# Layer 0 self attention: key norms and choice rounds in three pieces, two padding rows, rotation ahead of the output's norm, the next stage's second norm tile by tile

## The chip, the core and the metric

The kernel runs on one core of a Trainium2 chip. TensorE (PE) does the matrix products, with weight loads shown apart as PEld; VectorE (DVE), ScalarE (ACT) and GpSimd (POOL) do the rest; transfers are issued by SyncE (SP). The metric is the time of one execution in microseconds (us), as the median of several. A difference of about 0.3% is what a measurement of this kernel can tell from none.

## The reference, cut to what matters

A two-layer perceiver on `x` (64 batches of 32 rows of 256: 2048 rows) with a context of 64 x 257 rows of 64. Each layer is cross attention, self attention and a feed-forward part; each reads a layer norm of `x` and adds its result to `x`. The change lies in layer 0's self attention and in what is prepared there for later parts.

```python
xn = _layernorm(x, g_norm)          # of a layer-normed x: two norms in a row
q = xn @ Wq ; k, v = split(xn @ Wkv)        # 16 heads of 128, one k and one v
q = l2norm(q * 16) * 4 ; k = l2norm(k) * 4
attn = softmax(q @ k.T) ; out = (attn @ v) @ Wout
x = x + _layernorm(out, g_out)
# layer 0's feed-forward: the 4 likeliest of 16 blocks per row
prob = softmax(xf @ Wr.T + br) ; _, idx = top_k(prob, 4)
h = gelu(xf @ W1.T) * mask(idx) ; y = h @ W2.T
# layer 1's cross attention rotates the context
kv_rope = kv_c * cos + rotate_half(kv_c) * sin
```

## The kernel before, in words

All 2048 rows lie in SBUF as 16 tiles `xs[0]` to `xs[15]` of 128 rows (four batches each); four tiles make a group g = 0 to 3. Stages follow each other: A (layer 0 cross attention), B (layer 0 self attention, lines 845 to 1127), C (feed-forward), then layer 1. All that changes is in stage B, except that `pad` was allocated once for the whole kernel.

**Stage B is a loop over slots t = 0 to 16** (line 1077 on). In it the instructions of PE, DVE, ACT and POOL stand in the order in which the code writes them (`manual_schedule`), and each engine works its own list strictly in that order. The order of the transfers on SP's queue is chosen by the framework's own planner, not by the program text. Slot t does, for its tile:

- `similar(t)`: PE makes the scores `Sb` (L908) and, from the squares `q2b`, the query norms `ssb` (L916); ACT takes the root into `rqb` (L925).
- `gather(t-1)`: PE multiplies the last tile's weights with v into `avb` (L955); DVE and ACT copy two quarters each into `oTb` (L960, L962).
- `scale(t)`: DVE takes the reciprocal `rqb` (L930), then multiplies the scores into `pTb` (L932); `power(t)`: exponential on ACT (L936).
- `square(t+1)`: POOL squares queries of the next tile into `q2b` (L896, four instructions), as soon as ACT has copied them to `qTb` (L885).
- `project(t-1)`: PE, 32 passes into `yb` (L968); `norm_stats(t-1)`: DVE's statistics of `yb` (`lnb_bo`, L174), ACT's root (L980).
- `share(t)`: PE makes the denominators `denb` (L942), DVE their reciprocal `rdb` (L944) and the product `pTb` (L945), which the next slot's `avb` needs.
- `norm_out(t-1)`: DVE's reciprocal (L986) and `ynb` (L992); POOL multiplies by the gain (L993) and adds to `x` (L994).
- `rotate(t)`: nine POOL instructions (L822 to L839) rotate one sixteenth of the context for layer 1; SP stores the results (`ctd` L832, `nad` L840). `fetch(t+1)`: SP loads the next sixteenth (L804 to L812) into tiles with one buffer.
- `write_pad(t)`: DVE fills a row of padding (`pad`, L137 and L138) and SP stores it eight times to `srt` (L140, 1040 KB), for the experts of layer 1.

Four query products `qb` (L877, 8 passes each) per slot, ten ahead of use, fill PE at places 0 to 3. Further work is pinned by hand with `at(slot, place, fn)`: place 5 stands between `power` and `project`, place 3 behind `share`, place 4 behind `fetch`. Pinned there: `keys_norm(g)` (slots 3 and 6, place 5: the two norms in a row of four tiles, for the keys and queries of groups 2 and 3); the choice of blocks: `choose_norm`, `choose_turn`, `choose_blocks`, the four rounds `choose_best` (L679 to L692: largest, equal, first of the equal, strike out) and `choose_store` (PE transposes, L699; DVE copies, L701; SP stores `maskd`, L702); stage C's first hidden group (`hp`, `hc`, L716 to L724, slots 13 to 15) and output (`yc`, L731, L738, slots 15 and 16); and the norm of tiles 4 to 7 for stage C's second group, `ln_group(1, "c")` at slot 15 place 4, turned by `tp_c` (L244) at slot 16.

Helpers: `stats` (L174, L175: two DVE instructions), `ln_out` on ACT (L196), `rstd_of` (L156 to L168: by DVE, an ACT root and a DVE reciprocal, or on POOL by a power of -0.5, L159 and L160).

Of the kernel before, what the change touches and what calls it, by code (L numbers as in the profile page):

```python
# [7 lines left out]
F32 = mybir.dt.float32  # L8
AF = mybir.ActivationFunctionType
ALU = mybir.AluOpType  # L10
# [3 lines left out]
P = 128  # L14
B, S, D = 64, 32, 256
NT = B * S // P
NG = NT // 4
# [8 lines left out]
DP = D + 4  # L26
FE = 1024
EPS = 1e-5
# [19 lines left out]
def perceiver_kernel(ctx: ExitStack, tc: tile.TileContext, a: dict, out: bass.AP):  # L48
    nc = tc.nc


    const = ctx.enter_context(tc.tile_pool(name="const", bufs=1))
# [24 lines left out]
    xs = [x[:, :D] for x in xf]  # L77
# [51 lines left out]
    caus = cst[:, C_CAUS : C_CAUS + S]  # L129
    desc = cst[:, C_DESC : C_DESC + 16]  # L130

    pad = const.tile([P, DP], F32, name="pad")

    def write_pad(n_):


        nc.vector.memset(pad, 0.0)  # L137
        nc.vector.memset(pad[:, D : D + 1], 2.0 * B * S)  # L138
        r0 = n_ * NE * P
        nc.sync.dma_start(  # L140
            srt[r0 : r0 + NE * P].rearrange("(j p) c -> p j c", p=P), bc(pad, 1, NE)
        )
# [4 lines left out]
    mhalf = const.tile([P, 4], F32, name="mhalf")  # L147
# [22 lines left out]
    def stats(mv_slot, src, name, sign=None):  # L170
        st = sm(f"lnb_{name}", [P, 6])
        if sign is not None:
            nc.vector.tensor_copy(st[:, 0:1], sign)
        nc.vector.bn_stats(st, src)  # L174
        nc.vector.bn_aggr(mv_slot, st)  # L175
# [16 lines left out]
    def ln_out(x_, rs, sh, i, name, act=False):  # L192

        y = xnp.tile([P, D], F32, tag="xn", name=f"xn_{name}_{i}")
        if act:
            nc.scalar.activation(  # L196
                y, x_, AF.Identity, scale=rs[:, i : i + 1], bias=sh[:, i : i + 1]
            )
        else:
            nc.vector.scalar_tensor_tensor(  # L200
                y,
                x_,
                rs[:, i : i + 1],
                sh[:, i : i + 1].to_broadcast([P, D]),
                ALU.mult,
                ALU.add,
            )
        return y

    def ln_group(g, name, twice=False, act=False, power=False, sign=None):  # L210

        mv = sm(f"lnm_{name}{g}", [P, 4, 2])
        for i in range(4):
            stats(mv[:, i, :], xs[4 * g + i], f"{name}{g}_{i}", sign)
        rs, sh = ln_scale(mv, f"{name}{g}", twice, power)
        return [ln_out(xs[4 * g + i], rs, sh, i, f"{name}{g}", act) for i in range(4)]
# [132 lines left out]
    def keys_norm(g):  # L349
        latT[g] = ln_group(g, "b", twice=True, act=True, power=g == 0)  # L350
# [324 lines left out]
    def choose_best(g, work, rounds):  # L675

        lg, mx, mask = choice[g]
        for r in rounds:
            nc.vector.tensor_reduce(mx, lg, AX.X, ALU.max)  # L679
            eq = work.tile([P, 4, 16], F32, tag="eq", name=f"eqc{g}_{r}", bufs=1)  # L680
            nc.vector.tensor_tensor(eq, lg, bc(mx, 2, 16), ALU.is_equal)
            nc.vector.tensor_tensor(eq, eq, bc(desc, 1, 4), ALU.mult)
            m2 = sm(f"m2c_{g}_{r}", [P, 4])
            nc.vector.tensor_reduce(m2, eq, AX.X, ALU.max)
            one = mask
            if r:
                one = work.tile([P, 4, 16], F32, tag="one", name=f"onec{g}_{r}", bufs=1)
            nc.vector.tensor_tensor(one, eq, bc(m2, 2, 16), ALU.is_equal)
            if r < 3:
                nc.vector.scalar_tensor_tensor(lg, one, -2.0, lg, ALU.mult, ALU.add)  # L690
            if r:
                nc.vector.tensor_add(mask, mask, one)  # L692

    def choose_store(g, ps, work):

        mask = choice.pop(g)[2]
        mT_ps = ps.tile([16, 512], F32, tag="mm", name=f"mTp{g}")
        for i in range(4):
            nc.tensor.transpose(mT_ps[:, i * P : (i + 1) * P], mask[:, i, :], ident)  # L699
        mT = const.tile([16, 512], F32, tag="mT", name=f"mTc{g}", bufs=1)  # L700
        nc.vector.tensor_copy(mT, mT_ps)  # L701
        nc.sync.dma_start(maskd[g], mT)  # L702
# [23 lines left out]
    def output(g, hs, i, ps, tag, between=lambda f: None):  # L726
        y_ps = ps.tile([P, D], F32, tag=tag, name=f"yc{g}_{i}")
        for f in range(8):
            if f % 4 == 0:
                between(f // 4)  # L730
            nc.tensor.matmul(  # L731
                y_ps,
                hs[f][:, i * P : (i + 1) * P],
                c_2[:, f, :],
                start=(f == 0),
                stop=(f == 7),
            )
        nc.vector.tensor_add(xs[4 * g + i], xs[4 * g + i], y_ps)  # L738
# [106 lines left out]
    with tc.tile_pool(name="wB", bufs=2) as work, tc.tile_pool(  # L845
# [137 lines left out]
        def norm_out(t):  # L983
            y_ps, mv, sd = outs.pop(t)
            rs = sm(f"lnr_bo{t}", [P, 1])
            nc.vector.reciprocal(rs, sd)  # L986

            last = t == NT - 1
            yn = (xnp if last else work).tile(
                [P, D], F32, tag="xn" if last else "yn", name=f"ynb{t}"  # L990
            )
            nc.vector.tensor_scalar(yn, y_ps, mv[:, 0, 0:1], rs, ALU.subtract, ALU.mult)  # L992
            nc.gpsimd.tensor_tensor(yn, yn, vec[:, V_GOUT : V_GOUT + D], ALU.mult)  # L993
            nc.gpsimd.tensor_tensor(xs[t], xs[t], yn, ALU.add)  # L994
# [18 lines left out]

        steps = {}

        def at(slot, place, fn):
            steps.setdefault((slot, place), []).append(fn)

        for g in range(1, NG):
            at(4 * g - 4, 2, lambda g=g: keys_turn(g, ps2))
            slot, place_ = (0, 5) if g == 1 else (4 * g - 3, 1)
            at(slot, place_, lambda g=g: keys_of(g, ps2, 0))
            at(4 * g - 3, 3, lambda g=g: keys_of(g, ps2, 1))
            at(4 * g - 2, 2, lambda g=g: turn_keys(g, ps2))
            if g > 1:
                at((3, 6)[g - 2], 5, lambda g=g: keys_norm(g))
        for g in range(NG - 1):
            at(4 * g + 5, 5, lambda g=g: choose_norm(g))  # L1030
            at(4 * g + 6, 1, lambda g=g: choose_turn(g, ps2, work))
            at(4 * g + 7, 5, lambda g=g: choose_blocks(g, ps2, work))
            if g < NG - 2:
                at(4 * g + 7, 5, lambda g=g: choose_best(g, work, (0, 1)))
            at(4 * g + 8, 5, lambda g=g: choose_best(g, work, (2, 3)))
            if g < NG - 2:
                at(4 * g + 9, 2, lambda g=g: choose_store(g, ps2, work))
        ff, late = {}, []

        def ff_late():  # L1040
# [11 lines left out]

        def ff_output(i):
            output(0, [ff["h"][:, f, :] for f in range(8)], i, ps2, "mm")

        def spread(g):
            mb = []
# [13 lines left out]
        for i, (slot, place) in enumerate(((15, 3), (15, 3), (16, 0), (16, 1))):  # L1071
            at(slot, place, lambda i=i: ff_output(i))
        at(15, 3, lambda: choose_best(NG - 2, work, (0, 1)))
        at(15, 4, lambda: ff.update(xn1=ln_group(1, "c", act=True)))
        at(16, 2, lambda: ff.update(xT1=transposed(ff["xn1"], ps2, 1, "c")))

        for t in range(NT + 1):


            parts = [AHEAD + 4 * t + z for z in range(4)]  # L1080

            def place(z):
                if z < 4:
                    query_part(parts[z])
                for step in steps.get((t, z), ()):
                    step()

            if t < NT:
                similar(t)
            place(0)  # L1090
            if t > 0:
                gather(t - 1)
            if t < NT:
                scale(t)
            place(1)
            square(t + 1)
            ff_late()
            place(2)
            if t < NT:
                power(t)  # L1100
            ff_late()
            place(5)
            if t > 0:
                project(t - 1)
                norm_stats(t - 1)
            if t < NT:
                share(t)
            place(3)
            ff_late()
            if t > 0:  # L1110
                norm_out(t - 1)
            if t < NT:
                rotate(t, work)
            if t + 1 < NT:
                fetch(t + 1, work)
            place(4)
            if t == 2:
                numbers = all_numbers(counted)
                tri, one, token, base = (numbers[z] for z in ("tri", "one", "token", "base"))
                ntile, n128e, n128h = (numbers[z] for z in ("ntile", "n128e", "n128h"))  # L1120
            if t > 2:
                for t_ in {3: (0, 1), NT: (NT - 2, NT - 1)}.get(t, (t - 2,)):
                    nc.gpsimd.tensor_copy(xf[t_][:, D : D + 1], token[:, t_ : t_ + 1])
            write_pad(t)
            if t in (2, 4):
                load_c(t // 4)
        xT_c1 = ff["xT1"]
# [1420 lines left out]
```

## Time and profile before

| | |
|---|---|
| median of 3 runs | 1155.41 us (1152.88 to 1157.0) |
| profiled execution | 1160.48 us, its span 1158.6 us |
| busy share of the span | PE 96%, DVE 66%, ACT 50%, POOL 39% |
| stage B, slots 0 to 16 | 148 to 490 us of the span |
| PE busy in 148 to 490 us | 330.58 of 342 us |

Slot t is counted here from its reciprocal `rqb` on DVE. These start at 148.0, 165.5, 185.3, 206.4, 224.7, 244.4, 266.0, 285.9, 307.6, 327.4, 349.5, 369.3, 390.4, 410.1, 430.0 and 449.7 us (slots 0 to 15); slot 16 has none and is counted from 470. In an instruction line the first number is the start in us, the second the duration; `[x <-E tile L]` says that the engine had been idle for x us and what ended that. In a line of stretches each engine has its busy time and, in brackets, the instructions in it; then come the granted clock of TensorE, the share of DMA time and GB/s.

### The profile page before, as it was taken

What the parts mean: (1) busy time and instruction counts of PE and PEld (TensorE: products, weight loads), DVE (VectorE), ACT (ScalarE), POOL (GpSimd) and SP (SyncE); (2) the same over time, 40 slices, a digit from 0 to 9 for tenths busy, and PEclk for the clock granted to TensorE, in tenths of its full rate; (3) what the DMA queues carried; (4) which work ended last, traced back from release to release, by engine and by line L of the source; (5) the groups of instructions that cost most, each with busy time, mean ns of one, the idle gap of its engine ahead of it and who ended that gap; (6) DMA issues with size and microseconds to landing.
All of it is one profiled execution on the core that took longest, in us unless ns stands there. A gap on an engine that the chain in (4) does not pass through costs nothing. (4 is left out here: it accounts for less than half of the span.)

```text
span 1158.6 us, 26394 instructions
## 1 busy us (share of the span) xinstructions
PE 1106.6 (96%) x10026; PEld 790.2 (68%) x10026; DVE 769.7 (66%) x1812; ACT 575.4 (50%) x1442; POOL 457.0 (39%) x766
## 2 busy tenths in 40 slices
PE   9999999899999999999998999999999989889997
PEld 5667766677767657667676777777777657555653
DVE  5786246868987987765215787777878565765532
ACT  2346363545355365231227777777777456542221
POOL 1444255777768787410001121121222356732111
PEclk9999999999999999999999999999999998989999
DMA  5131132546346446492213121223230044212413
GB/s 133 57 95 40 33 88 85 171 123 168 97 129 206 116 116 191 144 278 69 74 39 66 29 56 29 74 56 83 56 83 19 4 133 126 86 35 74 153 38 118
DMA packets 98990, 109.05 MB, mean 94 GB/s; under 512 B 37240, under 2 KB 73465, under 8 KB 98642
## 3 DMA queue, kind: packets, MB, share of 16 engines
q1 hardware_dynamic: 97138, 103.05, 31.5%
q0 software_dynamic: 1728, 4.33, 1.1%
q8 instruction: 80, 1.31, 0.5%
q14 instruction: 44, 0.36, 0.1%
HBM read 76.36 MB, written 31.41 MB: 93 GB/s over the span
## 5 line engine op out<-in xcount | busy, mean ns | idle before, releaser
L1469 ACT ACTIVATE pp<-Sd,nm 128x256 f32<-128x256 f32 x256 | 119.9, 482 | 40.4 <-POOL nm L1466 40.4
L877 PE MATMUL qb<-xT_b,b_q 128*128 128x256 f32 x512 | 122.2, 386 | 0.8 <-ACT qTb L885 0.8
L877 PEld LDWEIGHTS qb<-xT_b,b_q 128*128 128x128 f32 x512 | 94.9, 191 | 40.1 <-issue 19.3
L1465 DVE TENSOR_REDUCE nm<-Sd 128x2 f32<-128x512 f32 x128 | 79.5, 684 | 54.1 <-PE Sd L1452 54.1
L968 PE MATMUL yb<-b_o,oTb 128*128 128x256 f32 x512 | 114.9, 383 | 0.5 <-DVE oTb L960 0.5
L1466 POOL TENSOR_SCALAR nm<-nm 128x2 f32<-128x2 f32 x128 | 27.0, 211 | 221.6 <-DVE nm L1465 221.3
L968 PEld LDWEIGHTS yb<-b_o,oTb 128*128 128x128 f32 x512 | 97.2, 192 | 14.7 <-issue 1.6
L1487 DVE TENSOR_TENSOR pp<-pp,rd 128x512 f32<-128x512 f32 x128 | 89.6, 700 | 4.4
L1497 PE MATMUL pt<-cst,pp 128*128 128x128 f32 x512 | 68.3, 275 | 6.2 <-DVE pp L1487 5.2
L1503 ACT COPY pTd<-pt 128x512 f32<-128x512 f32 x128 | 68.8, 591 | 10.4 <-PE pt L1497 4.8
L896 POOL TENSOR_TENSOR q2b<-qTb 128x512 f32<-128x512 f32 x64 | 64.7, 1041 | 13.9 <-ACT qTb L885 13.9
L1497 PEld LDWEIGHTS pt<-cst,pp 128*128 128x128 f32 x512 | 59.4, 141 | 15.7 <-ACT ld L1477 5.0
L885 ACT COPY qTb<-qb 128x512 f32<-128x512 f32 x64 | 37.3, 584 | 63.9 <-PE qb L877 61.1
L930 DVE RECIPROCAL rqb<-rqb 128x512 f32<-128x512 f32 x16 | 53.5, 3344 | 17.1 <-ACT rqb L925 17.1
L1245 PE MATMUL qd<-xT_d,d_m 128*128 128x256 f32 x256 | 63.8, 393 | 0.7 <-DVE rd L1486 0.3
L1544 PE MATMUL yd<-d_n,co 128*128 128x256 f32 x256 | 63.2, 391 | 0.0
L1478 POOL TENSOR_TENSOR sd<-sd,ld 128x2 f32<-128x2 f32 x128 | 27.4, 214 | 86.0 <-ACT ld L1477 86.0
L1452 PE MATMUL Sd<-ct,qTd 64*128 64x256 f32 x480 | 60.0, 388 | 0.0
L731 PE MATMUL yc<-c,hc 128*128 128x256 f32 x256 | 58.5, 382 | 0.0
L1518 PE MATMUL od<-pTd,na 128*64 128x256 f32 x480 | 58.4, 385 | 0.0
L1544 PEld LDWEIGHTS yd<-d_n,co 128*128 128x128 f32 x256 | 46.2, 189 | 16.7 <-DVE nm L1465 7.7
L944 DVE RECIPROCAL rdb<-denb 128x512 f32<-128x512 f32 x16 | 53.7, 3354 | 5.8 <-PE denb L942 5.6
(429 smaller groups left out, 2416.8 us busy)
## 6 DMA issues: line engine op xcount, KB each, us to landing
srt<-pad SPq DMA_DIRECT2D x17, 1040.0 KB
mb<-maskd SPq DMA_DIRECT2D x64, 128.0 KB
ct<-ctd SPq DMA_DIRECT2D x30, 257.0 KB
rct<-in_ctxT_dram SPq DMA_DIRECT2D x32, 128.5 KB
rrt<-in_ctxT_dram SPq DMA_DIRECT2D x64, 64.2 KB
ctd<-rct SPq DMA_DIRECT2D x32, 128.5 KB
nad<-rna SPq DMA_DIRECT2D x16, 256.0 KB
fg<-in_f_wg_dram SPq DMA_DIRECT2D x16, 256.0 KB
```

What stands on the lines that cost most here:

```text
L731: nc.tensor.matmul(y_ps, hs[f][:, i * P : (i + 1) * P], c_2[:, f, :], start=(f == 0), stop=(f == 7),)
L877: nc.tensor.matmul(q_ps[:, hh, :], b_q[:, k, h * P : (h + 1) * P], xT[:, k, c0 : c0 + 256], start=(k == 0), stop=(k == KC - 1),)
L896: nc.gpsimd.tensor_tensor(q2[:, 4 * h4 : 4 * h4 + 4, :], q, q, ALU.mult)
L968: nc.tensor.matmul(y_ps, oT[:, h, :], b_o[:, h, :], start=(h == 0), stop=(h == NH - 1))
L1245: nc.tensor.matmul(q_ps[:, r, :], m[:, k, pr * P : (pr + 1) * P], xT[:, k, c0 : c0 + 256], start=(k == 0), stop=(k == KC - 1),)
L1452: nc.tensor.matmul(logits[b][hh][:, u, :], qT[hs, b % 8, 4 * u : 4 * u + 4, :], ct[hs, b % 4, :KEYS], start=True, stop=True,)
L1465: nc.vector.tensor_reduce(nm, s_ps[hh], AX.X, ALU.max, negate=True)
L1469: nc.scalar.activation(pb[:, u, hh, :], s_ps[hh][:, u, :], AF.Exp, bias=nm[:, u : u + 1], accum_out=sd[:, u : u + 1],)
L1487: nc.vector.tensor_tensor(pp, pp, bc(rd, 2, KEYS), ALU.mult)
L1497: nc.tensor.transpose(pts[c][:, hh * 256 + u * P : hh * 256 + u * P + P], probs[b][:, u, hh, c * P : (c + 1) * P], ident,)
L1503: nc.scalar.copy(pT[:, c, :], pt)
L1544: nc.tensor.matmul(y_ps, co[:, pr, :], n[:, pr, :], start=(pr == pr0), stop=(pr == pr0 + n_pr - 1),)
```

## The change: what it does

Six edits, all in stage B:

1. `keys_norm(g)` for g = 2 and 3 becomes `keys_norm_step(g, z)`, one step per slot at place 5: slots 1, 2, 3 for g = 2 and 4, 5, 6 for g = 3. Both roots are taken on POOL (power of -0.5) and no longer on ACT. The last step holds the four `ln_out` on ACT, in the slot where they stood.
2. The four choice rounds of groups 0 and 1 stood two and two in slots 4g+7 and 4g+8; they stand now one, two, one in slots 4g+7, 4g+8, 4g+9. `choose_store` goes from slot 4g+9 to 4g+10, place 2. Group 2 keeps its rounds.
3. `pad` is no longer one row that lives through the kernel, but two rows in turn from stage B's pool.
4. `norm_out(t-1)` stands behind `rotate(t)` and `fetch(t+1)` instead of ahead of them.
5. `ln_group(1, "c")` at slot 15 is taken apart: the statistics of tiles 4 to 7 at place 4 of slots 11 to 14, scale and shift on POOL in slot 14, the four `ln_out` on ACT at slot 15, place 4.
6. The small tiles that must live through several slots come from stage B's pool.

```diff
-    pad = const.tile([P, DP], F32, name="pad")
-    def write_pad(n_):
+    def write_pad(n_, pool):
+        pad = pool.tile([P, DP], F32, tag="pad", name=f"pad{n_}")
         nc.vector.memset(pad, 0.0)
...
+        def keys_norm_step(g, z):
+            if z == 0:
+                mv = work.tile([P, 4, 2], F32, name=f"kbm_{g}", bufs=1)
+                for i in range(4):
+                    stats(mv[:, i, :], xs[4 * g + i], f"b{g}_{i}")
+                r1 = work.tile([P, 4], F32, name=f"kbr_{g}", bufs=1)
+                nc.gpsimd.tensor_scalar(r1, mv[:, :, 1], EPS, None, ALU.add)
+                nc.gpsimd.tensor_tensor(r1, r1, mhalf[:, 0:4], ALU.pow)
+                begun[g] = mv, r1
+            elif z == 1:
+                mv, r1 = begun[g]
+                r2 = work.tile([P, 4], F32, name=f"kbq_{g}", bufs=1)
+                nc.vector.tensor_tensor(r2, mv[:, :, 1], r1, ALU.mult)
+                nc.vector.tensor_tensor(r2, r2, r1, ALU.mult)
+                nc.gpsimd.tensor_scalar(r2, r2, EPS, None, ALU.add)
+                nc.gpsimd.tensor_tensor(r2, r2, mhalf[:, 0:4], ALU.pow)
+                begun[g] = mv, r1, r2
+            else:
+                mv, r1, r2 = begun.pop(g)
+                nc.vector.tensor_tensor(r2, r2, r1, ALU.mult)
+                nc.vector.scalar_tensor_tensor(r1, mv[:, :, 0], -1.0, r2, ALU.mult, ALU.mult)
+                latT[g] = [ln_out(xs[4 * g + i], r2, r1, i, f"b{g}", True) for i in range(4)]
...
-                at((3, 6)[g - 2], 5, lambda g=g: keys_norm(g))
+                for z in range(3):
+                    at((1, 4)[g - 2] + z, 5, lambda g=g, z=z: keys_norm_step(g, z))
...
-            if g < NG - 2:
-                at(4 * g + 7, 5, lambda g=g: choose_best(g, work, (0, 1)))
-            at(4 * g + 8, 5, lambda g=g: choose_best(g, work, (2, 3)))
-            if g < NG - 2:
-                at(4 * g + 9, 2, lambda g=g: choose_store(g, ps2, work))
+            if g == NG - 2:
+                at(4 * g + 8, 5, lambda g=g: choose_best(g, work, (2, 3)))
+                continue
+            for z, rounds in enumerate(((0,), (1, 2), (3,))):
+                at(4 * g + 7 + z, 5, lambda g=g, rounds=rounds: choose_best(g, work, rounds))
+            at(4 * g + 10, 2, lambda g=g: choose_store(g, ps2, work))
...
+        def second_stats(i):
+            if i == 0:
+                for z, shape in (("1m", [P, 4, 2]), ("1r", [P, 4]), ("1h", [P, 4])):
+                    ff[z] = work.tile(shape, F32, name=f"c{z}", bufs=1)
+            stats(ff["1m"][:, i, :], xs[4 + i], f"c1_{i}")
+            if i == 3:
+                rs, sh = ff["1r"], ff["1h"]
+                nc.gpsimd.tensor_scalar(rs, ff["1m"][:, :, 1], EPS, None, ALU.add)
+                nc.gpsimd.tensor_tensor(rs, rs, mhalf[:, 0:4], ALU.pow)
+                nc.gpsimd.tensor_tensor(sh, rs, ff["1m"][:, :, 0], ALU.mult)
+                nc.gpsimd.tensor_scalar(sh, sh, -1.0, None, ALU.mult)
+
+        def second_out():
+            return [ln_out(xs[4 + i], ff["1r"], ff["1h"], i, "c1", True) for i in range(4)]
...
-        at(15, 4, lambda: ff.update(xn1=ln_group(1, "c", act=True)))
+        for i in range(4):
+            at(11 + i, 4, lambda i=i: second_stats(i))
+        at(15, 4, lambda: ff.update(xn1=second_out()))
...
             place(3)
             ff_late()
-            if t > 0:
-                norm_out(t - 1)
             if t < NT:
                 rotate(t, work)
             if t + 1 < NT:
                 fetch(t + 1, work)
+            if t > 0:
+                norm_out(t - 1)
             place(4)
...
-            write_pad(t)
+            write_pad(t, work)
```

## The prediction on record

> **What bounds the kernel now.** The page's busy shares come first: PE 96% of the span, DVE 66%. So the question is where PE stands still. Stage B cut into its slots (start and end, length, then PE, PEld, DVE, ACT, POOL) shows it:
>
> ```profile
> 206.40:224.70 18.30, 15.89 (x80) 11.25 (x81) 17.02 (x31) 8.78 (x16) 11.57 (x13) 1.00 0.60 177
> ...
> 285.90:307.60 21.70, 20.02 (x109) 15.03 (x108) 20.09 (x33) 7.55 (x12) 14.34 (x16) 1.00 0.36 99
> 307.60:327.40 19.80, 19.11 (x99) 13.65 (x98) 18.96 (x27) 8.68 (x13) 15.63 (x18) 1.00 0.45 128
> 327.40:349.50 22.10, 22.10 (x112) 16.32 (x111) 17.09 (x32) 13.19 (x29) 16.89 (x18) 1.00 0.40 114
> ...
> 369.30:390.40 21.10, 19.84 (x108) 14.88 (x107) 19.73 (x33) 7.54 (x12) 14.10 (x16) 1.00 0.54 159
> 390.40:410.10 19.70, 19.36 (x100) 13.87 (x99) 18.86 (x28) 8.50 (x13) 15.53 (x17) 1.00 0.45 127
> 410.10:430.00 19.90, 18.64 (x86) 10.66 (x84) 16.67 (x29) 14.90 (x21) 17.43 (x18) 1.00 0.46 123
> ...
> 470.00:490.00 20.00, 18.67 (x78) 13.27 (x76) 16.62 (x50) 5.38 (x11) 11.57 (x13) 0.91 0.39 123
> ```
>
> These are slots 3, 7, 8, 9, 11, 12, 13, 16. Length minus PE is PE's gap: 2.4 us in slot 3, 1.7 in 7, 1.3 in 11, none in 9. All of stage B holds 342.0 - 330.6 = 11.4 us of gaps, so filling them can win no more. In slots 3, 7, 8, 11 and 12 DVE idles only 0.8 to 1.6 us: it sets the pace there, or nearly. The list of PE's waits in stage B (total, times, longest) names the instruction:
>
> ```profile
> PE avb L955 <- DVE pTb L945: 5.1, 3, 2.2
> PE ssb L916 <- POOL q2b L896: 1.5, 3, 0.8
> PE tp_c L244 <- DVE x L738: 1.0, 1, 1.0
> ```
>
> The three waits of `avb` are in slots 3, 7 and 11: place 5 (`keys_norm(2)`, 210.4 to 217.4; the choice with two rounds in 7 and 11) makes `pTb` late. The same `keys_norm` in slot 6 ends no wait of PE. What a round costs is seen in the timeline of slot 8 (start, duration):
>
> ```profile
> 315.65 1.05 DVE L681 TENSOR_TENSOR eqc<-lgc,mxc 128x64 f32<-128x64 f32 x1
> 316.69 1.26 POOL L839 TENSOR_TENSOR rna<-rna,rlb 128x512 f32<-128x512 f32 x1
> 316.73 1.30 DVE L682 TENSOR_TENSOR eqc<-eqc,cst 128x64 f32<-128x64 f32 x1
> 318.07 0.22 DVE L684 TENSOR_REDUCE m2c<-eqc 128x4 f32<-128x64 f32 x1
> ```
>
> The same L682 takes 0.22 us elsewhere; here it ends as POOL's instruction ends. A DVE instruction with two inputs seems to wait for the POOL instruction under way; the reduction, with one, does not. Slot 8's two rounds hold 9 such instructions, with durations 0.80, 0.65, 0.40, 1.31, 0.21, 1.05, 1.30, 0.84 and 0.96: mean w = 0.84.
>
> **The parts, step by step.** Times are of the profiled execution, 1160.48 us (span 1158.6 and 1.9 around it); that is 5.1 above the median 1155.41, and I carry the difference over to the median.
>
> *Key norms.* Slot 3 loses its seven microseconds at place 5 and keeps two small instructions (0.2 to 1.3 each). `yb` is done at 213.8, `denb` at 214.6; then `rdb` (3.35) and `pTb` (0.69) end by 218.8, before PE arrives at 220.15. The wait goes: **-2.2**. The statistics (four times 0.4 + 0.18 = 2.3) land in slots 1 and 4; in slot 1 DVE idles 5.3 before `lnb_bo`, which hides them, and slot 4 has 8.7 idle in all. Slot 2 idles 5.1; slot 5 gets only two multiplications under a PE that is busy throughout (21.60 of 21.60). Without such cover the 2.3 would be lost twice. POOL adds four times 0.23 + 1.04 (rows L159, L160): in slots 1, 2, 4, 5 `rotate`, `norm_out` and the next `square` queue behind it. POOL idles 89.3 in stage B before `ynb`, so this is covered.
>
> *Choice rounds.* Slot 7 drops a round of 2.8 (297.40 to 300.18): `lnb_bo` moves up to the end of `yb`, and the wait of 1.7 goes; in slot 11 likewise 1.3: **-3.0**. Slots 8 and 12 get rounds 1 and 2 in place of 2 and 3: one striking-out (L690) more, so 10 instructions of w and four reductions of 0.25. From one `avb` to the next `pTb`, DVE's chain in slot 8 was 324.96 - 305.06 = 19.90, 8.49 of it rounds; it becomes 11.41 + 1.0 + 10w = 20.8, against 19.99 from `avb` to `avb`: +0.8. Slot 12 likewise: 407.62 - 388.07 = 19.55, less 8.32, plus 1.0 + 10w: 20.6 against 19.63, +1.0. Slot 13 gets round 3 (4w + 0.5) and slot 12's late statistics (0.6), and loses the copy L701 (0.67): 425.31 - 407.70 = 17.61 becomes 21.4 against 19.91, +1.5. `choose_store` takes PE's 0.6 from a slot that DVE now paces to slot 14, which PE paces: +0.6. Slots 9 and 10, with PE busy 22.10 of 22.10 and 19.56 of 19.80, hide theirs; slot 9's DVE has 5.0 idle for 3.9. Together 24w - 16.25: **+3.9**.
>
> *Rotation ahead of the output's norm.* POOL no longer holds the rotation (10.4 us) until `ynb`, 89.3 us of idling over 16 slots. The squares come next after `norm_out`, ten microseconds earlier, and the waits of `ssb` go: 0.2 in slot 4; the 0.5 and 0.8 in slots 8 and 13 buy nothing where DVE paces. **-0.2**. POOL needs 1.5 + 4.1 + 10.4 = 16.0 of about 20 us per slot. The transfers of `fetch` follow the rotation on SP: 7 us of issue, of which the first rotation needs 3. They start about four microseconds before the next `ynb`, and 5.6 of norm and squares stand ahead of their use: covered. If not, squares have another 8 us before `ssb`.
>
> *Second norm by tiles, end of the stage.* Slot 15 ends with 4.1 us of statistics, ACT's root and shift on DVE (471.08 to 475.17); the `oTb` copies and `x` wait behind them:
>
> ```profile
> 475.21 2.08 ACT L196 ACTIVATE xn_c<-x,lnh_c,lnr_c 128x256 f32<-128x256 f32 x4 [0.93 <-DVE lnh_c L189]
> 476.05 0.62 PE L244 MATMUL tp_c<-cst,xn_c 128*128 128x128 f32 x2 [1.00 <-DVE x L738]
> 478.40 3.77 PE L968 MATMUL yb<-b_o,oTb 128*128 128x256 f32 x11
> ```
>
> With the `xn_c` of ACT made earlier, PE goes from its last `yc` (475.05) through eight transposes (1.1) into `yb` at 476.2: 2.2 less, of which I count 1.6 until the buffers are passed on. And the clock: the next stretch is
>
> ```profile
> 478.00:482.00 4.00, 4.00 (x14) 3.34 (x13) 3.86 (x7) 1.23 (x3) 3.77 (x5) 0.64 0.80 237
> ```
>
> Granted 0.64, just after 1.3 us of gaps in 474 to 478: 4.0 x 0.36 = 1.4 us lost. I count it as filled with the gap: **-3.0** in all. Bounds: -1.6 if the clock falls anyway; -3.6 at best. The four `stats` in slots 11 to 14 (0.6 each) follow `pad`, where DVE waits for `avb` (1.8 idle before `oTb` in slot 14, 1.4 in slot 10); slot 12's is counted above. POOL's two new products lie between 0.2 (L159) and 1.04 (L160), off the path.
>
> The Trainium skill (TensorE: Matmul & The Clock Gate, Part 1) lets the clock fall only after a whole idle window of about 3.4 us; this trace has it fall after 1.3 us of gaps. By that rule the fall has nothing to do with the gap, and the sum would be 1.4 us poorer.
>
> *Two padding rows.* Nothing in stage B waits for the one row's store, so: 0. From above: the last store is issued at 490.13, behind 2 MB of `d_q`. If a tile of stage C lay on the row it would wait for 3 MB at 320 GB/s (490 to 495), some 10 us. By the order of first use, 80 KB of each partition in stage B's pools stand ahead of the row, and stage C's tiles come to 58 KB.
>
> **Sum.** -2.2 - 3.0 + 3.9 - 0.2 - 3.0 = -4.5: the profiled execution 1156.0, the median 1150.9.
>
> **Rivals.**
> A, forecast: 1150.9, own range 1146.3 (w = 0.22, the shortest row, by the same formulas with PE as floor: -9.1) to 1151.9 (0.3% below).
> B, the gaps move: w near 0.95 (losses 6.5) gives -1.9; or new gaps in slots 8, 12 and 13 draw the clock down twice (1.4 each), -1.7. For it: DVE is busy 18.9 of 19.8 in these slots. 1153.5, at most 1158.
> C, slower: the later rounds lie wholly under the rotation, which now begins after the squares. With w = 1.31 (longest row) losses are 24 x 1.31 - 16.25 = 15.2, net +6.8: 1162.2. It decides from w = 1.03 on, and passes 0.3% at 1.17. Against it: slot 8 was already under rotation and squares.
> D, a tile of stage C waits for the padding: -4.5 + 10 = +5.5, 1160.9.
>
> The Trainium skill (SBUF — State Buffer, Who interferes with whom) has the later of two such instructions blocked for the whole of the other. Where each moved instruction meets a fresh POOL instruction this speaks for C.
>
> **Numbers.** A 0.60, B 0.21, C 0.13, D 0.06. Differences over 0.3% are what a measurement of this kernel can tell from none: faster 0.60 (A), same 0.21 (B), slower 0.19 (C, D). The range goes from A's best, 1146.3, to B's end, 1158; C and D stay outside.
>
> **What would show it.** Right: no `avb` wait in slots 3, 7, 11; new ones of about 1 us in slots 8, 12, 13; `ssb` without waits; `ynb` on POOL hardly waited for; clock 1.0 and no `tp_c` wait at the end of the stage. Wrong: mean w over 1.03, a fetch that POOL waits for, a gap of PE at the start of stage C.

## The result, and the profile after

The changed kernel takes 1165.42 us (median of 4 runs, 1164.89 to 1166.73) against 1155.29 us (median of 4, 1152.88 to 1157.0) before: ratio 1.0079, 95% interval [1.0053, 1.0105]. It is **slower by 0.8%**, where 0.4% faster was forecast, and 7 us above the upper end of the range. Its profiled execution took 1165.57 us (span 1163.8). That is only 5.1 above the profiled execution of before, which was 5.2 above its own median; so the comparison is made place by place. The changed kernel has one line less ahead of stage B: L716 of before is L715 here.

TensorE's waits of the changed kernel from 130 to 520 us (total, times, longest):

```profile
PE hp L715 <- ACT hc L722: 6.8, 2, 6.5
PE avb L954 <- DVE pTb L944: 6.5, 3, 3.9
PE yb L967 <- DVE oTb L959: 1.5, 1, 1.5
PE kvp L363 <- ACT qTb L884: 1.1, 1, 1.1
```

The waits of `ssb` and `tp_c` of before are gone, as forecast. But one wait of 6.5 us is new, at `hp`, and the longest at `avb` is now 3.9 where it was 2.2.

The stretches of slots 3, 7, 8, 9, 12, 13, 14 of the changed kernel, counted from `rqb` as before (length, then PE, PEld, DVE, ACT, POOL, granted clock):

```profile
206.96:222.99 16.03, 15.80 (x80) 11.23 (x81) 11.24 (x16) 7.67 (x13) 13.05 (x16) 1.00 0.73 223
283.79:303.56 19.77, 19.77 (x108) 14.89 (x107) 16.60 (x26) 7.76 (x12) 15.42 (x17) 1.00 0.44 128
303.56:324.28 20.72, 19.16 (x100) 13.92 (x99) 19.91 (x28) 8.67 (x13) 14.16 (x16) 1.00 0.45 129
324.28:347.17 22.89, 21.80 (x108) 15.98 (x107) 20.12 (x37) 12.85 (x29) 16.87 (x19) 1.00 0.40 118
387.65:408.75 21.10, 19.54 (x102) 14.25 (x101) 20.36 (x31) 8.47 (x13) 14.54 (x16) 1.00 0.50 140
408.75:431.19 22.44, 18.32 (x72) 9.82 (x70) 21.54 (x35) 13.81 (x19) 15.88 (x17) 0.96 0.39 115
431.19:454.73 23.54, 23.29 (x90) 13.13 (x90) 16.24 (x21) 13.49 (x18) 16.81 (x17) 0.90 0.37 107
```

Slot 7 now has no gap on PE (19.77 of 19.77). Slots 8 and 12 have some 1.6 us of gaps each, with DVE idle for only 0.8: DVE paces them. Slot 13 has 4.1 us of gaps, and slot 14 is long although PE is busy in nearly all of it: its clock is 0.90, so its matrix products themselves are slow.

**Where the 6.5 us come from.** The start of stage C in the timeline of the changed kernel (start, duration; ACT's gelu needs a table first):

```profile
491.56 0.39 SPq L139 DMA_DIRECT2D srt<-pad  x1
...
496.60 1.28 ACT L722 ACT_TABLE_LOAD   x1 [6.55 <-DMA srt<-pad]
...
498.55 1.22 PE L715 MATMUL hp<-xT_c,c 128*128 128x512 f32 x1 [6.54 <-ACT hc L722]
```

ACT stands 6.55 us until the store of the last padding row has landed; PE's buffers for `hp` are full, so it stands too. Within this gap the clock falls too, from 494.07 for 10.2 us. Three stretches of four microseconds show it:

```profile
494.00:498.00 4.00, 0.00 (x0) 0.00 (x0) 3.46 (x14) 1.39 (x2) 0.50 (x1) 0.51 0.50 164
498.00:502.00 4.00, 3.46 (x4) 1.51 (x5) 2.55 (x10) 0.98 (x2) 1.61 (x2) 0.50 1.04 358
502.00:506.00 4.00, 4.00 (x8) 1.77 (x7) 0.93 (x2) 1.19 (x2) 0.00 (x0) 0.71 1.21 322
```

**Where slots 13 and 14 lose.** VectorE and TensorE in slot 13:

```profile
415.36 1.31 DVE L681 TENSOR_TENSOR eqc<-eqc,cst 128x64 f32<-128x64 f32 x1
...
420.64 1.16 DVE L162 TENSOR_SCALAR lnv_r<-lnm_r 128x4 f32<-128x4 f32 x1
...
427.18 0.69 DVE L944 TENSOR_TENSOR pTb<-pTb,rdb 128x512 f32<-128x512 f32 x1
```
```profile
427.92 1.13 PE L954 MATMUL avb<-pTb,kvb 32*128 32x512 f32 x6 [3.88 <-DVE pTb L944]
429.29 2.07 PE L954 MATMUL avb<-pTb,kvb 32*128 32x512 f32 x2 [0.24 <-ACT rqb L924]
```
```profile
430.00:434.00 4.00, 4.00 (x11) 2.06 (x10) 4.00 (x4) 3.27 (x6) 4.00 (x6) 0.50 0.86 281
```

Round 3 of group 1 stands here in one list with group 2's own norm (`lnb_r`, `lnv_r`, 418.4 to 423.1); behind both comes `pTb`, for which PE waits 3.88 us. Then TensorE runs at half its clock, from 429.22 for 6.8 us. The last two passes of `avb` come later still, behind ACT's `rqb`.

**All slots.** The table gives the time from the first `avb` of a slot to the first `avb` of the next (slot 16: to stage C's first `hp` after it; "C": from there to its first `yc`), less the same of before, each from the timeline of one profiled execution, in us. Slots 1, 2, 5, 6 and 15 differ by 0.03 at most everywhere. The kernels are those of the experiments below.

| slot | before | changed | one row, const | group 1's rounds back | both rounds back | choice alone | rotation alone | 2nd norm alone | keys alone |
|---|---|---|---|---|---|---|---|---|---|
| 3 | 20.97 | -1.19 | -1.18 | -1.19 | -1.16 | 0.00 | -0.65 | 0.03 | -2.23 |
| 4 | 19.75 | -0.43 | -0.43 | -0.42 | -0.42 | 1.27 | -0.42 | 0.00 | -0.42 |
| 7 | 21.53 | -1.75 | -1.75 | -1.75 | -0.36 | -1.75 | -0.18 | 0.06 | -0.35 |
| 8 | 19.99 | 0.73 | 0.74 | 0.73 | 1.62 | 0.52 | 1.97 | 0.02 | -0.35 |
| 9 | 22.04 | 0.84 | 0.84 | 0.83 | 1.68 | -0.43 | 1.65 | 0.00 | 0.01 |
| 10 | 19.87 | 0.84 | 0.84 | 0.84 | -0.01 | 0.83 | -0.01 | 0.00 | 0.00 |
| 11 | 21.11 | -1.33 | -1.33 | -0.01 | 0.00 | -1.33 | -0.02 | 0.03 | 0.00 |
| 12 | 19.63 | 1.08 | 1.08 | 1.97 | 2.00 | 4.57 | 1.97 | 0.01 | 0.03 |
| 13 | 19.91 | 2.01 | 2.00 | -1.01 | 0.64 | 1.36 | -1.01 | 0.22 | 0.23 |
| 14 | 19.76 | 4.69 | 4.43 | 0.06 | 0.46 | 3.39 | 0.06 | 0.00 | 0.00 |
| 16 | 16.73 | -3.59 | -3.58 | -3.59 | -3.59 | 0.24 | -2.29 | -1.31 | -0.53 |
| C | 14.42 | 8.97 | -0.12 | -0.12 | -0.12 | 0.01 | 0.00 | 0.00 | -0.12 |
| sum | | +10.9 | +1.5 | -3.7 | +0.7 | +8.7 | +1.1 | -1.0 | -3.7 |

The sum of the changed kernel, +10.9, agrees with the difference of the medians, +10.1. The two profiled executions differ by 5.1 only, because what follows the first `yc` of stage C took 652.0 us in the changed kernel's and 657.2 in that of before. That remainder varies between executions, from 651.9 to 659.4 in the 16 kernels profiled here (658.1 in the changed kernel with only its last padding row elsewhere), so the effect of the change is read from the rows above.

### The profile page after: what moved, and what is told of

Same layout as the page of the kernel before. It is cut to its first block, busy times and chain, and to the rows that moved or that the text cites. A ratio compares the mean times of both kernels' runs of the same rounds, so it can differ in the third digit from the quotient of the medians.

```text
span 1163.8 us, 26379 instructions
## 1 busy us (share of the span) xinstructions
PE 1107.4 (95%) x10026; PEld 789.2 (68%) x10026; DVE 766.4 (66%) x1801; ACT 574.6 (49%) x1437; POOL 464.1 (40%) x778
## 3 DMA queue, kind: packets, MB, share of 16 engines
q8 instruction: 80, 1.31, 0.5%
```

## The experiments

Each ratio is to the kernel before, run on the same chip, with its 95% interval. Two theories stood at first. **P**: the padding rows come from a pool that closes with stage B; the first write into stage C's pool waits for the last row's store, and this costs some 9 us. Its rival **R**: the rotation's new place costs the time, by transfers that start together, and the rows cost nothing. A further theory, **Q**, was about what is left besides: round 3 in slot 13 makes `pTb` late, and the clock falls behind the gap. The program as built speaks for P: ACT's first write of stage C, the tile `hc` at byte 99,040 of a partition, lists waits for the stores of the rows of slots 14, 15 and 16. It doesn't lie on them: the rows are at bytes 144,992 and 146,048, and the tiles of stage C's pool end near 122,600.

### The row alone, both ways

The changed kernel with one row that lives on, and the kernel before with only the rows changed:

```diff
# one row, const
+    pad = const.tile([P, DP], F32, name="pad")
-        pad = pool.tile([P, DP], F32, tag="pad", name=f"pad{n_}")
# rows only, on the kernel before: the reverse
```

> The changed kernel, but with the padding row as before: one row that lives through the whole kernel. Theory P (stage C's first write by ACT waits for the store of the last padding row, because the row now belongs to stage B's pool): the wait of 6.5 us before the first gelu of stage C goes, with it the half clock that follows it; 9.0 us less than the changed kernel, about 1156.4. Rival R (the rotation's new place costs the time, by transfers that start together): about 1165, and the wait of ACT stays, for another transfer.

> The kernel before with one edit: two padding rows from stage B's pool. Theory P: 7 to 9 us slower than before, 1162 to 1164, and PE idle for some 6 us at the start of stage C. Rival R: no change, 1155.

Measured: 1156.96 us, ratio 1.0004 [0.9987, 1.0021]; and 1166.14 us, ratio 1.0081 [1.0057, 1.0105]. The row alone takes the kernel before to where the change took it, and without it the change is neither gain nor loss. Counted as in the table, row C of the kernel with the rows alone is +8.45; its slot 4 is +1.26, by a fall of the clock that the last section explains. The wait stands in the list of ACT's waits of the second kernel, from 484 to 506 us, and is in none of the first:

```profile
ACT L722 <- DMA srt<-pad: 6.8, 1, 6.8
```

P holds, and R falls: the wait goes with the row. But the forecast's gain doesn't come back with it: without the row the slots sum to +1.5, not to -4.5. The experiments below look for that rest.

### Only the last row from elsewhere

```diff
+        if n_ == NT:
+            pad = const.tile([P, DP], F32, name="padlast")
+        else:
             pad = pool.tile([P, DP], F32, tag="pad", name=f"pad{n_}")
```

> The changed kernel with two rows from stage B's pool for slots 0 to 15 and only the last padding row, slot 16's, a tile that lives through the kernel. Theory P in its narrow form (what costs is the one store that is issued as stage B ends): ACT's wait of 6.5 us at the start of stage C goes and the time is that of the run with the row put back, within 1 us of 1157. Rival (rows in the stage's pool cost something throughout, or the store before it, issued 15 us earlier, is waited for as well): 1161 to 1166, with a wait left.

Measured: 1159.25 us, ratio 1.0000 [0.9984, 1.0016]; row C, counted as in the table, is -0.13, as with one row. So it is the last row's store alone that is late; the others have long landed.

### The choice rounds put back, wholly and in group 1

Both with one const row.

```diff
# both rounds back: the four lines of the change, undone. Group 1's:
+            if g == 1:
+                at(4 * g + 7, 5, lambda g=g: choose_best(g, work, (0, 1)))
+                at(4 * g + 8, 5, lambda g=g: choose_best(g, work, (2, 3)))
+                at(4 * g + 9, 2, lambda g=g: choose_store(g, ps2, work))
+                continue
```

> The changed kernel with the padding row and the choice rounds as before. Theory Q (round 3 in slot 13 makes the softmax product late there, a gap of 3.9 us on PE, and the clock halves after it, 6.7 us together): slot 13 has no gap, slots 7 and 11 have their old waits of 1.7 and 1.3 us; the gains of slot 3 (2.1) and of the end of the stage (3.6) stay: 1155.3 - 5.7 = 1149.6. Rival (rounds moved cost nothing in themselves, the clock falls at chance): as the run with the row alone put back, 1156.

> The changed kernel with the padding row as before and only group 1's choice rounds put back (two and two, stored in slot 13); group 0 keeps one, two, one in slots 7 to 9, where slot 9 has room on DVE. Theory Q: slot 7's wait gone, slot 8 up to 1.4 later, slot 11's wait back, nothing lost in slot 13: 1149 to 1150. Rival: as the run with the row alone put back, 1156.

Measured: 1155.19 us, ratio 0.9983 [0.9966, 1.0001], and 1153.25 us, ratio 0.9973 [0.9954, 0.9992]. The first is a miss: slots 13 and 14 do get their time back, but slots 8, 9 and 12 get longer than in the changed kernel, by 0.8 to 0.9 each. Something other than the moved rounds makes them long. The second falls short of its 1149 to 1150 as well, since slot 12 is +1.97 where nothing was expected. It shows what group 1's rounds cost together with their clock: the slots' sum falls from +1.5 to -3.7, by 5.2 us (the two medians, 1156.96 and 1153.25, differ by 3.7).

### Each part alone

Four kernels, each the kernel before with one of the diff's parts and nothing else.

> The kernel before with one edit: the output's norm stands behind the rotation. Forecast's reasoning: the waits of the query norms on the squares go, 0.2 to 1.5 us in all; nothing else: ratio 0.999 to 1.000. Rival (the squares now run while DVE makes the table of numbers in slot 2 and copies the context, and block it): 1 us slower in slot 3, ratio 1.000 to 1.001.

> The kernel before with one edit: the second norm of stage C by tiles. Reasoning: slot 16 shorter by 3.0 to 3.6 us (less 0.5 for the statistics in slot 13, where DVE has room): ratio 0.997. Rival (the gain at the end came with the earlier rotation, which leaves DVE undisturbed there): 1.6 us or less, ratio 0.9985 or more.

> The kernel before with one edit: key norms in three steps. Reasoning: the 2.2 us wait in slot 3 goes, nothing is lost elsewhere: ratio 0.998. Rival (the powers on POOL push the rotation and the squares back, as norm, rotation and squares still stand in the old order): the waits of the query norms on the squares grow in slots 1, 2, 4 or 5 and take 1 us or more of it back: 0.999 or more.

> The kernel before with the choice rounds of groups 0 and 1 over three slots alone: the order of rotation and output's norm, the padding row, the key norms and the second norm are as before. This prices the choice by itself. Theory (the rounds cost where they go to, and round 3 of slot 13 stops TensorE): slots 7 and 11 1.3 to 1.8 us shorter each; slots 9 and 10 0.8 longer each or more (round 3 ahead of the choice's norm, store of the mask one slot later); slot 13 2 longer and slot 14 2 to 5 longer (a gap of over 3 us in front of avb, then half a clock): sum +3 to +5, ratio 1.003 to 1.005. Slots 8 and 12 tell who makes them long: at 0 to +0.3 each it is the rotation alone, which meets the rounds only when it runs ahead of the output's norm; at +0.7 to +1.0 as in the changed kernel, the later round as well. The prediction on record has this part at -3.0 +3.9 = +0.9 us and no clock change: ratio 1.0008.

Measured: rotation 1160.79 us, 1.0009 [0.9989, 1.0028]; second norm 1157.8 us, 0.9999 [0.9982, 1.0016]; keys 1154.47 us, 0.9961 [0.9947, 0.9976]; choice 1165.2 us, 1.0074 [1.0050, 1.0099].

The **rotation alone** makes slots 8 and 12 longer by 1.97 each, which neither side of its expectation had. Its timeline in slot 8, to be held against the same instructions of before (the prediction's third view):

```profile
305.25 4.04 POOL L896 TENSOR_TENSOR q2b<-qTb 128x512 f32<-128x512 f32 x4
...
309.24 1.28 POOL L822 TENSOR_TENSOR rct<-rct,cst 128x514 f32<-128x514 f32 x1
...
318.26 1.28 POOL L839 TENSOR_TENSOR rna<-rna,rlb 128x512 f32<-128x512 f32 x1
```
```profile
309.30 1.29 DVE L681 TENSOR_TENSOR eqc<-lgc,mxc 128x64 f32<-128x64 f32 x1
310.63 1.12 DVE L682 TENSOR_TENSOR eqc<-eqc,cst 128x64 f32<-128x64 f32 x1
...
318.30 1.33 DVE L692 TENSOR_TENSOR maskc<-maskc,onec 128x64 f32<-128x64 f32 x1
```

Before, GpSimd did the same in the other order:

```profile
307.67 1.26 POOL L822 TENSOR_TENSOR rct<-rct,cst 128x514 f32<-128x514 f32 x1
...
318.04 4.03 POOL L896 TENSOR_TENSOR q2b<-qTb 128x512 f32<-128x512 f32 x4
```

There the rotation began at 307.67, four microseconds ahead of the rounds, and the last instructions met the squares. Now the squares come first, and the two rounds, 309.30 to 319.63, begin with the rotation and lie wholly under it, 309.24 to 319.54. Their nine instructions with two inputs take 9.52 us instead of 7.52: the whole 1.97. In the changed kernel the last of the four rounds left for slot 9; ten such instructions are left in slot 8, and they take 8.54.

The **choice alone** was expected at +3 to +5 and came to +8.7. Of this, +1.27 in slot 4 is a fall of the clock in a slot that this edit doesn't touch. What the expectation had not seen is slot 12, +4.57, in the timeline of that kernel:

```profile
384.91 0.54 SPq L140 DMA_DIRECT2D srt<-pad  x1
...
390.60 0.28 DVE L137 MEMSET pad<- 128x260 f32 x1 [7.98 <-DMA srt<-pad]
```

The store of slot 10's padding row is issued at 384.91 here, right behind loads (`mb`) that read the mask which the choice has stored; before it was issued at 370.98. DVE waits 7.98 us for it before it may fill the one row again, and `oTb` and PE's `yb` wait behind that. That the mask's later store moved the row's in the queue is likely and not shown by itself. A second row would cover this wait; with all parts together and one row it does not come up (first experiment).

The **second norm alone** gives 1.3 of the 3.6 at the end of the stage, as the rival in its expectation had it; the rotation alone gives 2.3. The **keys alone** have the whole -2.2 in slot 3 and another 1.8 in slots 4, 7, 8, 16 and row C that nobody had forecast; with 0.4% off, they are the best of the parts.

### Parts together

Since the changed kernel holds two gains, one loss and one part that is both, the question was whether the gains can be had alone.

```diff
# v1: the kernel before with key norms and second norm as changed
# v3, v5, v6: v1 with the order turned in slots NT - n to NT - 1 alone, n = 1, 3, 2
-            if t > 0:
+            if 0 < t < NT - n or t == NT:
                 norm_out(t - 1)
             if t < NT:
                 rotate(t, work)
             if t + 1 < NT:
                 fetch(t + 1, work)
+            if NT - n <= t < NT:
+                norm_out(t - 1)
# v4: v3 with rounds 0 | 1, 2, 3 in slots 4g + 7 | 4g + 8, groups 0 and 1
```

> The kernel before with the two parts that cost nothing anywhere: key norms over three slots and the second norm by tiles; choice rounds, rotation and padding row as before. By the slots of the two parts run alone: slot 3 -2.2, slot 4 -0.4, slots 7 and 8 -0.35 each, end of the stage -1.3 to -1.8, slot 13 +0.2: sum -4.4 to -4.9, ratio 0.9958 to 0.9962. If instead the parts take each other's gain at the end of the stage: 0.997.

> The kernel before with key norms, second norm by tiles, and the rotation ahead of the output's norm in slot 15 only, not in the other slots. Theory (the early rotation pays at the end of the stage, where it frees VectorE for the last rounds, and costs 2 us each in slots 8 and 12, where the rounds come to lie under it): slots 8 and 12 stay where key norms alone leave them, end of the stage -3.6: sum about -6.8, ratio 0.994. Rival (the gain of the end comes from every earlier slot being ahead): end of the stage -1.3 to -1.8 only, ratio 0.996.

> The third of these with one edit more: of the choice of groups 0 and 1, round 0 stays in slots 7 and 11, and rounds 1, 2, 3 go to slots 8 and 12; nothing goes to slots 9 and 13, and the mask is stored where it was. Theory (with the rotation behind the output's norm VectorE has room in slots 8 and 12, where two rounds cost nothing before): slots 7 and 11 -1.75 and -1.3, slots 8 and 12 0 to +1.0 each, no gap in slot 13: 1 to 3 us below the third, ratio 0.992 to 0.993. Rival (a third round there costs what it did in slot 13, and stops TensorE for over 3 us): slots 8 and 12 or the ones behind them +2 to +7 each, ratio 0.997 to 1.003.

Measured: v1 1151.57 us, 0.9953 [0.9935, 0.9972], by slots -4.9: the parts add up. v3 1152.1 us, 0.9958 [0.9937, 0.9979]: a miss, the end of the stage gains 0.3 and not 3.6. v4 1156.54 us, 0.9993 [0.9973, 1.0013]: a miss, slots 7 and 11 do give back 1.75 and 1.33, but slots 8, 9 and 12 come to +1.90, +1.62 and +2.25 (with falls of the clock at 322.3 and 407.6): more than was gained.

Why v3's end did not gain is in its timeline: GpSimd's rotation and VectorE's second round in slot 15.

```profile
461.75 1.27 POOL L822 TENSOR_TENSOR rct<-rct,cst 128x514 f32<-128x514 f32 x1 [3.07 <-issue]
```
```profile
468.11 1.31 DVE L682 TENSOR_TENSOR eqc<-eqc,cst 128x64 f32<-128x64 f32 x1
```

The input of slot 15's rotation is fetched only after slot 14's rotation is through (456.6), so GpSimd idles 3.07 us and starts 18 us after the slot's first `avb` (the profile names no releaser; the loads' issue from 457.0 to 463.0 fits). It then falls on the first two rounds, where it fell on the last two before, and PE's `tp_c` waits 3.2 us in all for `x`. The order has to be turned some slots ahead.

> The kernel before with key norms, second norm by tiles, and the rotation ahead of the output's norm in slots 13, 14 and 15. Theory A (a rotation can start only when its inputs are there, some 17 us after the rotation before it; so the order pays at the end of the stage only if two slots or more are ahead, and slots 8 and 12, whose rounds must not meet it, keep the old order): end of the stage -3.3 to -3.6, slots 3, 4, 7, 8 as in the kernel with key norms and second norm, slot 13 -1.0 to +0.3: sum -6.5 to -8, ratio 0.993 to 0.9945. Theory B (what the order gains at the end comes from all the slots ahead of it): end of the stage -0.3 to -1.8, ratio 0.995 to 0.997.

> The same in slots 14 and 15 only. Theory A: the rotation of slot 15 ends before the last two rounds begin, but may meet the first two: end of the stage -2.3 to -3.6, ratio 0.993 to 0.9955. Theory B: -0.3 to -1.8, ratio 0.995 to 0.997.

Measured: v5 1151.89 us, 0.9937 [0.9914, 0.9960]; v6 1150.26 us, 0.9924 [0.9902, 0.9945]. The end of the stage gains 3.58 and 3.59, slots 8 and 12 keep what they have in v1, and the sums are -6.9 both. VectorE in v6, in the choice's last two rounds:

```profile
471.48 0.22 DVE L682 TENSOR_TENSOR eqc<-eqc,cst 128x64 f32<-128x64 f32 x1
...
473.81 0.22 DVE L692 TENSOR_TENSOR maskc<-maskc,onec 128x64 f32<-128x64 f32 x1
```

0.22 us each: slot 15's rotation ended at 465.9. Theory A holds: two slots are enough. The runs don't tell v5 and v6 apart. v6 has the lowest ratio found, 0.76% below the kernel before; by the two ratios, 1.5% below the changed one.

## Why the prediction was wrong

It found TensorE's gaps and priced most of them well; one step failed outright, and three were mis-sized.

**The failed step: "Two padding rows ... 0", "If a tile of stage C lay on the row".** What was wrong is the assumption that only an overlap makes a wait. In the program as built the first write into the next stage's pool waits for every tile of the closed pool, the stores that read them too. The price in rival D, +10, was near the measured +9.0 (6.5 of gap, the rest clock), but D had 0.06 and the wrong condition, and the range left it out. The prediction's own sign of being wrong, "a gap of PE at the start of stage C", is what came. That the closed pool, and not some other rule, sets this wait is read from the program's list of waits and from the addresses; no run here tells it apart by itself.

The sum over the layout holds for the pools that it counted. It left out `d_q`, weights for layer 1 that are loaded as stage C begins: in the changed kernel they lie at bytes 135,136 to 151,520, over both rows, and their load is issued at 496.34, behind the row's store, where it was issued at 487.22 before. This overlap is real, but it isn't what stops ACT, whose list of waits has the stores and not `d_q`, and no loss behind stage C is seen for it (the 652.0 us above).

**Mis-sized: slots 13 and 14, +1.5 and +0.6, measured +2.0 and +4.7.** The step "17.61 becomes 21.4" was good to half a microsecond. What it left out is the clock: it counted the clock's fall at the end of the stage as a gain and not the same fall as a loss behind a new gap of 3.9 us. Rival B had it at 1.4 a time; here it costs 3.4, half of the 6.8 us that the low clock lasted. Of slot 14's +4.7, 0.6 is the moved store, and the last 0.7 fits the two late passes of `avb`.

Slot 9, put at 0 because "DVE has 5.0 idle for 3.9", measured +0.84 with slot 10 at +0.84 (of which 0.6 is the moved store of the mask, foreseen in slot 14 only). Round 3 stands ahead of the choice's norm there, so the root that ACT takes for that norm is later, and ACT's copy `qTb` behind it: PE's `kvp` waits 1.1. DVE's idle time was no full cover, because ACT's list is in order. But it takes both parts: with the choice alone slot 9 is 0.43 shorter. There the two-input instructions of round 3 take 2.99 us; in the changed kernel, where the rotation begins with them at 328.27, they take 4.38.

**Mis-sized: rotation, -0.2.** Alone it costs 2.0 in slots 8 and 12 each and 1.65 in slot 9 (there with a fall of the clock at 324.9), and gains 2.3 at the end. Rival C had the mechanism, "the later rounds lie wholly under the rotation, which now begins after the squares", and set against it that "slot 8 was already under rotation and squares". It was; but how long an instruction waits depends on where it meets GpSimd's, and w of the same nine went from 0.84 to 1.06. Nor is it two inputs that make an instruction wait: `lnv_r` (L162), with one, took 1.16 us in the view of slot 13 and ended at 421.80, GpSimd's product at 421.77; with GpSimd idle, at 498.10, it takes 0.15. The time that C gave (1162.2) asked for more than that.

**Right.** Mean w was forecast at 0.84 and measured at 0.85, 0.85 and 0.94 in slots 8, 12, 13: slots 8 and 12 came to +0.73 and +1.08 against +0.8 and +1.0. Slots 7 and 11: -1.75 and -1.33 against -1.7 and -1.3. The end of the stage: -3.59 against -3.0, bounds -1.6 to -3.6; clock 1.0 there. `ssb` has no wait left. Half right: POOL's wait for `ynb` fell from 89.3 to 60.6 us, where it was to be "hardly waited for", and the new gaps in front of `avb` are 1.3, 1.3 and 3.9 us, where about 1 each was forecast.

**Slot 3: -2.2, measured -1.2.** Alone the keys give -2.23. Together with the rotation, slot 2's `pTb` meets POOL's `rna` and takes 1.70 instead of 0.69; all behind it is 1.0 later, and `yb` waits 1.5. The step was right, and another part of the change took half.

So the forecast fails without the row, too. The steps then sum thus: -4.5 forecast, +4.6 for slots 13 and 14, +1.7 for 9 and 10, -0.6 at the end, +0.8 for slots 3 and 4, -0.1 for 7 and 11: +1.9, as the table's column of the changed kernel has it without row C (10.9 - 9.0).

## What to carry to other kernels

When a tile moves from a long-lived pool into one that closes, look for what still reads it at the close: here a store of 1 MB, late in its queue, held up the next stage's first write although it touched none of its memory. A new gap on TensorE is to be priced with the clock behind it, and idle time of the engine that gets more work is no cover if another engine's ordered list waits for its result. Before an order is turned everywhere for a gain in one place, ask which slots pay for it: turned in two slots instead of all, it kept the gain and dropped the cost.

## What the runs showed of the hardware

**The clock falls after gaps shorter than its own step, and not always.** In each execution all stretches of half clock begin on one grid of 3.41 us (in the changed kernel 118.61, 429.22 and 494.07: 91 and 19 steps apart). But for the last of an execution they last 3.4, 6.8 or 10.2 us, and the grid lies elsewhere in each execution. The same gap of 2.2 us in slot 3 had full clock behind it in the kernel before, and a stretch of 3.4 us at half clock from 219.6 in the kernel with the choice alone. Both from 218 to 222 us, before first:

```profile
218.00:222.00 4.00, 2.15 (x12) 1.44 (x8) 3.93 (x4) 3.25 (x8) 0.00 (x0) 1.00 0.46 92
```
```profile
218.00:222.00 4.00, 3.65 (x14) 2.40 (x15) 3.74 (x8) 1.07 (x2) 2.82 (x4) 0.70 0.86 285
```

The gap of 3.9 us in slot 13 drew 6.8 us of half clock in all three kernels that had it. The Trainium skill (TensorE: Matmul & The Clock Gate, Part 1) has a free-running window of 3413 ns, with which the grid agrees; its rule that the clock falls after at least one idle window does not hold for the 2.2 us.

**What goes with a fall is how much idle time lies in one step of the grid.** In the kernel with the choice alone this gap, 216.18 to 218.35, lies whole in the step from 216.17 to 219.58. In the kernel before, a step ends at 221.44 and cuts the gap (220.15 to 222.31) into 1.29 and 0.87. Counted from 145 to 510 us in all 16 executions, over the steps that begin at full clock: of 11 in which TensorE stood idle for 2.0 us or more, each had half clock behind it; of 1630 with less than 1.1 us, none; of the 52 between, 6.

**One gap can thus cost 0 or 1.3 us by where the grid lies** (slot 4: +1.27 with the choice alone, 0.00 with the second norm alone, behind the same gap). This fits the spread of some microseconds among one kernel's runs, and that the difference of two profiled executions (5.1) and that of the medians (10.1) stand so far apart here; that it explains the whole of either is not shown.
